# Re-dealing the steps of a period in a fused GCN and graph-attention kernel

## The chip, the cores and the metric

The kernel runs on one core of a Trainium2 chip. The metric is the device time of one execution in microseconds; before the change it is 2834.84 us, the median of 3 runs (2834.20 to 2835.28). The core has five engines with a queue of instructions each[...]: TensorE (PE; its weight loads are shown as PEld), VectorE (DVE), ScalarE (ACT), GpSimd (POOL) and SyncE (SP), which here issues every DMA.

## The reference

64 graphs of 256 nodes with 512 features, all in float32. `adj` is 256x256 for each graph. First comes a three-layer GCN with a residual and a layer norm, then a graph attention with a residual and a layer norm:

```python
h = relu(adj @ (x @ W1) + b1)
h = relu(adj @ (h @ W2) + b2)
x = layernorm(x + adj @ (h @ W3) + b3)
q, k = split(x @ Wqk);  v = x @ Wv
w = mask / sqrt(512) * rowsum(q * (adj @ (k * mask)))
x = layernorm(x + softmax(w, axis=nodes)[:, :, None] * v)
```

## The kernel before

**Tiling.** Two graphs make a pair; there are 32 pairs. Every matrix product is done in the Strassen-Winograd form of `seven` (L110): seven products of half-size blocks instead of eight, numbered 1 to 7, with sums of blocks prepared before and results combined after. In each of its seven steps a group of matmuls writes a PSUM bank; ScalarE copies partial results into `tmp` tiles, VectorE (`add`, L65) or GpSimd (`padd`, L68) makes the block sums. One bank (`x` in `seven`) is added to by products 1, 6, 5 and 3, so each of them but the first must wait until ScalarE has copied out the one before; another (`v`) is used by 7 and then by 4, and 4 must wait until VectorE has done the sum called `c22`.

**The double product.** In the attention, q and k enter only as q·k, so Wq and Wk are multiplied together once at the start (`make_m`). Then x is multiplied by that matrix and by Wv with two nested Strassen forms, 49 products of 128x128 blocks (`attention`, L512). The outer products are dealt into four groups a, b, c, d (`OUTER`, L213). The order is a and b by turns, seven steps each, and then c and d by turns (`STEPS`). The weights for this do not stay on the chip: `fetch` (L225) loads them from DRAM into a ring of 7 slots, 256 KB for a step of a, b or c, and 128 KB for one of d. Each step, after its matmuls, issues the fetch for the step seven further on (L545). The text calls these 28 steps the products p1 to p28, and the fetch for p(n) f(n).

**Periods and steps.** The work of three pairs overlaps. A period `i` runs generators that each yield after a small piece of work, and a string, `ORDER`, says which generator makes its next step (`run`, L631). There are 31 periods with `ORDER` (i from 1 to 31), one with `START` ahead of them and one with `END` behind. Every engine executes its own instructions in the order in which this string issued them, so the string is the schedule. The k-th occurrence of a letter is the k-th step of that generator, and the text names it so (F23 is the 23rd F):

- F, `front` (L402) of pair i: F1 to F7 are the seven products with W1 (L306), F8 to F11 the four groups of adj products with relu (L328, ScalarE L331), F12 to F18 the products with W2, F19 to F22 adj again, F23 to F29 those with W3. F8 first issues the load of the next pair's transposed x (L75), and F23 first issues the load of `x` (L89, 1 MB), since `put["x"] = load_x(i)` stands right before its products. 4 matmuls each.
- B, `back` (L429) of pair i-1: B1 to B7 are the seven adj products of the third layer (L364, 2 matmuls each), with the residual added by GpSimd; B8 to B12 are the layer norm and a blockwise transpose on VectorE; B13 sends the result through DRAM (`via`) to get it transposed; B14 makes block sums on GpSimd (L97).
- G, `gather`: the seven products adj·x (L364, 2 matmuls each). After G7 the load of an adj for two pairs later is issued (L84, 512 KB, in the periods up to i = 30).
- M, `attention`: M1 makes the copies and sums Z (ScalarE L521, VectorE L524), M2 and M3 the sums I (GpSimd). M4 to M17 are p1 to p14 (groups a, b), M18 to M20 VectorE work in between, M21 to M32 and M36, M37 are p15 to p28 (groups c, d). M33, M34, M38, M39 are the scores of the softmax (VectorE L560), M35 and M40 sums of v.
- E, `finish` (L592) of pair i-2: E1 transposes the scores on TensorE (L383), takes the maximum (VectorE L385), the exponential (ScalarE L388) and scales it (VectorE L390, L391). E2 transposes back (L398) and scales v. E3 to E7 are the statistics of the last layer norm, E8 to E11 its application (L617); E10 and E12 first issue a store of half a pair (L620, 512 KB).
- S, `sums`: block sums of the next pair's x (S1 to S3, GpSimd L285 to L292), the bias b3 (S4 to S7, L68) and the block sums of adj (S8 to S11).

**Buffers concerned.** 8 PSUM banks and 6 `tmp` tiles for all of this. `x` and `xm` share one buffer: `x` can be loaded once the products of `xm` (G1 to G6) are done. `v` is one buffer: its new contents (M20) must wait for the two stores.

The lines that say when a fetch and the adj load are issued, and those around E1:

```python
                fetch(at[0] + RING)
```
```python
                if n == 6:
                    put["gt"] = gt
                    if i + 2 < NPAIR:
                        aTs[i + 2] = load_adj(i + 2)
```
```python
        nc.vector.tensor_reduce(nmax, pw, AX.X, OP.max, negate=True)
        nc.scalar.activation(e, pw, AF.Exp, bias=nmax, accum_out=tot)
        nc.vector.reciprocal(rtot, tot)
        nc.vector.tensor_scalar(e, e, rtot, None, op0=OP.mult)
```

Of the kernel before, what the change touches and what calls it, by code (L numbers as in the profile page):

```python
# [20 lines left out]
def gcn_then_graph_attention(ctx: ExitStack, tc: tile.TileContext, xT, xN, adjT, mask, W1, b1, W2, b2, W3, b3,  # L21
# [570 lines left out]
    def finish(i, prev, gs=range(G)):  # L592

        r, v, w = prev
        n = len(gs)
        sm = softmax_rows(w, gs)
        yield
        s = softmax_cols(sm, gs)
        for k, g in enumerate(gs):
            for h in range(NH):  # L600
                nc.vector.scalar_tensor_tensor(v[:, g, h], v[:, g, h], s[:, h, k:k + 1], r[:, g, h, :],
                                               op0=OP.mult, op1=OP.add)
        yield
        st = small.tile([P, NH, n, 6], FP, name="st")
        mvt = small.tile([P, NH, n, 2], FP, name="mvt")
        for k, g in enumerate(gs):
            for h in range(NH):
                nc.vector.bn_stats(st[:, h, k], v[:, g, h])
                yield
        for k in range(n):  # L610
            for h in range(NH):
                nc.vector.bn_aggr(mvt[:, h, k], st[:, h, k])
        rs, nb = inv_std(mvt, n)
        yield
        for k, g in enumerate(gs):
            for h in range(NH):
                nc.scalar.activation(v[:, g, h], v[:, g, h], AF.Identity, scale=rs[:, h, k:k + 1],  # L617
                                     bias=nb[:, h, k:k + 1])
                yield
            nc.sync.dma_start(out[i, :, g * NH * D:(g + 1) * NH * D].rearrange("p (h f) -> p h f", h=NH), v[:, g])  # L620

    ORDER = ("BFFFEFFEBEFBBBFBFBBFBFEFBFBFBEBBBGFEGSFFEGGFEGEEFEMFMFFFGMMGSMEMMMMMMMMMMMSMMMMMMFSM"
             "FMMFSMMMMFFSMMMSEMMSMFMFSMSMSMM")
    START = ("BFFBBFFFBFBBBBFBBFBBBBBBBFBFBBFFBBBBBBBFFBFBBBFBFBBFBBFBBBFFBFBBBBFBBFFBFBBBBBFSBBBB"
             "SSSBBFSSBSFSBSBSBBBSBSB")
    END = ("BEEBEEBEEBBBBEBBBBEBEEBBBGGEMMBBMGGMEMGMMGMBMMMGMMMMMMMMMMMMMMMMMMMMMMMMXMMMMMXXMMYX"
# [2 lines left out]
    def run(order, **gens):  # L631
        res = {}
        for k in order + "FSBGMEXY" * 90:
            if k in gens and k not in res:
                try:
                    next(gens[k])
                except StopIteration as e:
                    res[k] = e.value
        assert len(res) == len(gens)
        return res  # L640

    def later(put, f):
        yield from f(put)
# [5 lines left out]
    for i in range(NPAIR + 1):  # L649
# [12 lines left out]
        if i == NPAIR:  # L662
            for g, k in enumerate("XY"):
                gens[k] = later(done, lambda d, g=g: finish(NPAIR - 1, d[g], [g]))
        order = START if i == 0 else ORDER if i < NPAIR else END
        res = run(order.replace(" ", ""), **gens)
# [39 lines left out]
```

## Time and profile before

| what | value |
|---|---|
| time, median of 3 runs | 2834.84 us |
| span of the profiled execution | 2832.0 us |
| granted TensorE clock, mean | 0.995 |
| instructions | 36770, of these 12688 matmuls |
| DMA, mean of the span | 142 GB/s; 328.54 MB read, 72.48 MB written |
| fetches of the ring, 256 KB | 672, median 3.3 us from issue to landing |
| load of x, 1 MB | 32, median 6.5 us |
| load of adj, 512 KB | 32, median 5.3 us |
| store of half a pair, 512 KB | 64, median 3.7 us |
| matmul 128x256, float32 | shown as 379 ns each; two such instructions for each matmul of the program |

In the profile an engine's row lists what it did, and in brackets how long it sat idle before and what released it. Since matmuls overlap in the array, the shown duration of one is longer than the distance to the next; idle time of TensorE has therefore to be read from the distances between starts. A float32 matmul of the program appears as two matmul instructions.

### The profile page before, as it was taken

The numbers are of one execution on the slowest core, as the hardware profiler recorded it, in microseconds if no ns is written. First come the engines' busy times: TensorE is split into PE (matmuls) and PEld (weight loads), VectorE is DVE, ScalarE is ACT, GpSimd is POOL, SyncE is SP. The second block draws the span as 40 slices with busy tenths as digits, with TensorE's granted clock in tenths as the row PEclk, the third lists the DMA queues.
The fourth block names the chain that finished last, engine by engine and source line by source line (L and its number), as shares of the span: only waits on it lengthen the run. The fifth ranks groups of instructions, "written<-read, shape, count | busy, mean of one in ns | idle before, by whom it ended". The sixth has DMA issues, their size and how long they took to land.

```text
span 2832.0 us, 36770 instructions
## 1 busy us (share of the span) xinstructions
PE 2740.0 (97%) x12688; PEld 2371.6 (84%) x12688; DVE 1703.6 (60%) x2898; ACT 1151.9 (41%) x1888; POOL 1786.5 (63%) x1446
## 2 busy tenths in 40 slices
PE   9999999999999999999999999999999999999996
PEld 8888888888888888888888888888888888888875
DVE  4566555665556665556655566655566655666556
ACT  2343344433444433444334444334443334443343
POOL 2656665666756666656667566666565676666663
PEclk9999999999999999999999999999999999999998
DMA  6434554344544344543445433455434455334442
GB/s 218 143 120 136 159 172 141 107 140 146 158 155 126 117 147 149 171 141 109 140 143 159 156 127 116 143 159 166 143 113 136 142 158 164 123 114 149 144 151 95
DMA packets 197752, 403.45 MB, mean 142 GB/s; under 512 B 20160, under 2 KB 57408, under 8 KB 189504
## 3 DMA queue, kind: packets, MB, share of 16 engines
q1 hardware_dynamic: 197568, 401.10, 44.5%
q8 instruction: 103, 1.69, 0.2%
q14 instruction: 81, 0.66, 0.1%
HBM read 328.54 MB, written 72.48 MB: 142 GB/s over the span
## 4 chain that ended last, share of the span: by engine, by line
PE 86%; DMA 7%; ACT 3%; DVE 3%; issue 1%; POOL 0%; SPq 0%; ACTq 0%; DVEq 0%; POOLq 0%
PE ps L306 37%; PE ps L543 18%; PE ps L328 15%; PE ps L364 14%; DMA ring<-mv 6%; DVE e L391 1%; ACT L388 1%; ACT e L388 1%; ACT tmp L126 1%; ACT tmp L117 1%; PE ps L248 1%; PE ps L398 0%; DVE gt L560 0%; DMA xT<-in_xT 0%; DVE w L97 0%
## 5 line engine op out<-in xcount | busy, mean ns | idle before, releaser
L306 PE MATMUL ps<-w_T,S 128*128 128x256 f32 x2304 | 539.7, 379 | 3.0 <-POOL S L289 1.8
L65 DVE TENSOR_TENSOR R<-ps,tmp 128x512 f32<-128x512 f32 (+1 forms) x384 | 235.4, 620 | 455.1 <-PE ps L543 350.2
L306 PEld LDWEIGHTS ps<-w_T,S 128*128 128x128 f32 x2304 | 437.8, 190 | 63.5 <-POOL S L289 3.1
L543 PE MATMUL ps<-ring,I 128*128 128x256 f32 x1792 | 435.3, 383 | 36.5 <-DMA ring<-mv 33.8
L328 PE MATMUL ps<-aT,sup 128*128 128x256 f32 x2048 | 457.7, 379 | 0.0
L328 PEld LDWEIGHTS ps<-aT,sup 128*128 128x128 f32 x2048 | 389.5, 190 | 52.4
L543 PEld LDWEIGHTS ps<-ring,I 128*128 128x128 f32 x1792 | 332.8, 190 | 107.0 <-ACT tmp L134 40.3
L65 DVE TENSOR_TENSOR sup<-ps,tmp 128x512 f32<-128x512 f32 x288 | 195.6, 686 | 279.7 <-PE ps L306 171.5
L134 ACT COPY tmp<-ps 128x512 f32<-128x512 f32 (+1 forms) x288 | 158.3, 561 | 473.6 <-PE ps L306 251.3
L68 POOL TENSOR_TENSOR I<-Z 128x384 f32<-128x384 f32 (+1 forms) x128 | 173.3, 1374 | 262.6 <-ACT Z L521 244.9
L543 PE MATMUL ps<-ring,Z 128*128 128x256 f32 x1344 | 327.7, 380 | 0.0
L68 POOL TENSOR_TENSOR tmp<-tmp,R 128x512 f32<-128x512 f32 x192 | 214.9, 1140 | 169.8 <-DVE R L580 141.5
L126 ACT COPY tmp<-ps 128x512 f32<-128x512 f32 (+1 forms) x288 | 158.1, 560 | 358.9 <-PE ps L543 173.8
L117 ACT COPY tmp<-ps 128x512 f32<-128x512 f32 (+1 forms) x288 | 158.7, 563 | 326.7 <-PE ps L364 120.2
L543 PEld LDWEIGHTS ps<-ring,Z 128*128 128x128 f32 x1344 | 256.4, 191 | 34.7
L68 POOL TENSOR_TENSOR tmp<-tmp,x 128x512 f32<-128x512 f32 x96 | 120.9, 1273 | 208.8 <-ACT tmp L134 208.8
L306 PE MATMUL ps<-w,hT 128*128 128x256 f32 x1024 | 242.1, 379 | 0.0
L331 ACT ACTIVATE hT<-ps,b 128x512 f32<-128x512 f32 x256 | 167.6, 681 | 157.5 <-PE ps L328 155.1
L68 POOL TENSOR_TENSOR x<-x,b3b 128x512 f32<-128x512 f32 x128 | 176.8, 1382 | 73.2 <-DMA x<-in_xN 63.8
L306 PEld LDWEIGHTS ps<-w,hT 128*128 128x128 f32 x1024 | 194.7, 190 | 26.5 <-DVE R L65 0.3
L285 POOL TENSOR_TENSOR S<-hT 128x512 f32<-128x512 f32 x64 | 81.8, 1279 | 202.8 <-ACT hT L331 202.8
L364 PE MATMUL ps<-T,aS 128*128 128x256 f32 x768 | 204.6, 389 | 0.0
(111 smaller groups left out, 4503.8 us busy)
## 6 DMA issues: line engine op xcount, KB each, us to landing
ring<-mv SPq DMA_DIRECT2D x672, 256.0 KB, 3.3
x<-in_xN SPq DMA_DIRECT2D x32, 1024.0 KB, 6.5
out<-v SPq DMA_DIRECT2D x64, 512.0 KB, 3.7
xT<-in_xT SPq DMA_DIRECT2D x31, 1024.0 KB, 4.8
via<-tr SPq DMA_DIRECT2D x31, 1024.0 KB, 4.3
x1T<-via SPq DMA_DIRECT2D x124, 256.0 KB, 4.7
ring<-mv SPq DMA_DIRECT2D x224, 128.0 KB, 2.9
aT<-in_adjT SPq DMA_DIRECT2D x32, 512.0 KB, 5.3
```

The lines of the kernel that those rows point to most:

```text
L65: nc.vector.tensor_tensor(o, a, b, op=OP.add)
L68: nc.gpsimd.tensor_tensor(o, a, b, op=op)
L117: nc.scalar.copy(t1, x)
L126: nc.scalar.copy(u, x)
L134: nc.scalar.copy(q, x)
L285: eng.tensor_tensor(S[2], blk(0, 0), blk(1, 0), op=sub)
L306: nc.tensor.matmul(ps[:, g], lhsT=src[n][:, c, g], rhs=w[n][:, c], start=(first and g == 0 and c == 0), stop=(g == G - 1 and c == 1), skip ...
L328: nc.tensor.matmul(ps[:, g], lhsT=C[k][c // 2][:, g, (c % 2) * P:(c % 2 + 1) * P], rhs=aT[:, k, g], start=(g == 0 and k == 0), stop=(g == ...
L331: nc.scalar.activation(hT[c // 2][:, c % 2], ps, AF.Relu, bias=b[:, c:c + 1])
L364: nc.tensor.matmul(ps[:, g], lhsT=aS[n][:, g], rhs=mov[n][:, g], start=(first and g == 0), stop=(g == G - 1), skip_group_check=True)
L388: nc.scalar.activation(e, pw, AF.Exp, bias=nmax, accum_out=tot)
L543: nc.tensor.matmul(ps[:, k], lhsT=left[n](place[o]), rhs=wt[:, k], start=(first and k == 0), stop=(k == len(outer) - 1), skip_group_check= ...
```

## The change

Only the string `ORDER` changes. It holds the same steps, each letter equally often, in another order; `START` and `END` stay.

```diff
-    ORDER = ("BFFFEFFEBEFBBBFBFBBFBFEFBFBFBEBBBGFEGSFFEGGFEGEEFEMFMFFFGMMGSMEMMMMMMMMMMMSMMMMMMFSM"
-             "FMMFSMMMMFFSMMMSEMMSMFMFSMSMSMM")
+    ORDER = ("FBFEFFEFEBBBBFBBFBFBFBFFBBBFEFBEBGFSGFFGEGFEEGEEFEFFFEMMGGMFMMFMMMMMSMSMMMMMMMMMMFMS"
+             "MMFMMMMMFMMSESMSMSMFMSMSMMMFFSM")
```

Spelled out by steps:

- *The start of the double product.* F22 and F23 now stand amid the first steps of groups a and b: G6, G7, M3, F22, M4, M5, F23, M6 to M17. Before it was F22, G6, M3, M4, G7, M5 to M17, and F23 came only after M22. With F23 the load of x goes out between the fetches f9 and f10.
- *The adj load* (behind G7) is issued before M4 instead of after it, and *the second store* (E12) before M1 instead of after M5.
- *Z and I.* M1 and M2 come after F21 instead of around F19, and M3 before F22.
- *The softmax transposes.* F1, B1, F2, E1, F3, F4, E2, F5 instead of B1, F1, F2, F3, E1, F4, F5, E2.
- *The products of the back.* B2 to B7 stand closer together: B2, B3, B4, B5, F6, B6, B7, F7 instead of B2, F6, B3, B4, B5, F7, B6, F8, B7. B8 to B13 follow earlier, and E4 to E7 (statistics of the last layer norm) later.
- *The second half of the double product.* F24 now comes before M22, F25 before M25, F27 after M34 (it was before M30), and F28 and F29 after M39 (they were after M35 and M36).
- *The sums S.* S2 comes after M10 (it was after G7) and S3 after M11 (it was after M16); S4 to S11 are dealt anew, mostly a few steps earlier or later.

## The prediction

> **What bounds the kernel now.** I read the page first: shares of the span, then the chain that ended last.
>
> ```profile
> PE 2740.0 (97%) x12688; PEld 2371.6 (84%) x12688; DVE 1703.6 (60%) x2898; ACT 1151.9 (41%) x1888; POOL 1786.5 (63%) x1446
> PE 86%; DMA 7%; ACT 3%; DVE 3%; issue 1%; POOL 0%; SPq 0%; ACTq 0%; DVEq 0%; POOLq 0%
> ```
>
> TensorE is the bound, and the change removes none of its work. What can move is the idle time, so next come the waits of TensorE alone (engine, line, waited for: total us, times, longest):
>
> ```profile
> PE ps L543 <- DMA ring<-mv: 33.8, 39, 2.3
> PE ps L398 <- DVE e L391: 22.6, 28, 3.6
> PE ps L383 <- DVE gt L560: 9.4, 3, 4.0
> ```
>
> These are understated: a 128x256 matmul is shown as 0.379 us long, but the next one starts 0.216 us after it. I therefore added up, over the whole trace, every distance between matmul starts beyond 0.216. Inside line 543 that gives 52.9 us (52 in the periods of ORDER, 1.7 for each of the 30 that load an adj); ahead of line 398 it gives 21.1 us (0.7 a period). A period has 386 matmuls of 0.216 us, 83.5 us, plus about 0.4 for the four small transposes, and lasts 86.4 on average. So about 2.5 us a period, 77 us in 31 periods, is all there is to win, and those two waits are nearly all of it.
>
> The first wait, in one period. TensorE's timeline, then SyncE's (start, us, engine, line), then a piece of the chain of waits:
>
> ```profile
> 1082.46 1.89 PE L543 MATMUL ps<-ring,Z 128*128 128x256 f32 x8
> 1085.69 1.10 PE L543 MATMUL ps<-ring,I 128*128 128x256 f32 x4 [1.34 <-DMA ring<-mv]
> 1087.60 2.69 PE L543 MATMUL ps<-ring,I 128*128 128x256 f32 x11 [0.80 <-DMA ring<-mv]
> ```
>
> ```profile
> 1077.47 0.34 SPq L230 DMA_DIRECT2D ring<-mv  x1
> 1078.37 0.33 SPq L84 DMA_DIRECT2D aT<-in_adjT  x1
> 1079.20 0.32 SPq L230 DMA_DIRECT2D ring<-mv  x1
> 1079.61 0.38 SPq L620 DMA_DIRECT2D out<-v  x1
> 1080.09 13.83 SPq L230 DMA_DIRECT2D ring<-mv  x14
> ```
>
> ```profile
> 1080.09 7.38 DMA ring<-mv
> ```
>
> The ring holds 7 slots, so fetch f(n) is issued when product p(n-7) is done, and p(n) needs it. Ahead of f9 stands an adj load (0.5 MB), ahead of f10 an output store (0.5 MB): f10, issued at 1080.09, lands 7.38 us later, while p10 wanted it earlier. Fetches that follow land 0.67 us apart and are eaten one per 0.865 us, so the stall happens once and does not come back. The last period of ORDER, which has no adj load, lost 0.33 us there.
>
> The second wait (all engines, same columns):
>
> ```profile
> 1119.46 0.59 ACT L126 COPY tmp<-ps 128x512 f32<-128x512 f32 x1 [2.87 <-PE ps L306]
> 1119.68 0.41 DVE L385 TENSOR_REDUCE nmax<-ps 2x1 f32<-2x256 f32 x1
> 1120.07 1.28 ACT L388 ACT_TABLE_LOAD   x1
> 1121.36 0.47 ACT L388 ACTIVATE e<-ps,nmax 2x256 f32<-2x256 f32 x1
> 1122.14 1.44 DVE L391 TENSOR_SCALAR e<-e,rtot 2x256 f32<-2x256 f32 x1
> 1123.73 0.25 PE L398 MATMUL ps<-ident,e 2*128 2x2 f32 x2 [0.63 <-DVE e L391]
> ```
>
> The table load starts 0.02 us after the copy of line 126 in nearly every period, at times before nmax is ready, so it waits only for its place in ScalarE's queue. That copy needs F3, the product straight ahead of the transposes.
>
> **What the Trainium skill says.** "DMA: Bandwidth & Descriptors", section Queues, rings and completion order: all that SyncE issues goes through one row of rings, taken in order on each DMA engine. The trace agrees: f10 lands 0.6 us behind the store ahead of it. "ScalarE: Activation LUTs", section What ACT_TABLE_LOAD costs: about 1283 ns, and a drain of about 1380 ns. The load is 1.28 here; no separate drain shows, so I count 1.28. "SBUF — State Buffer", section SBUF: two separate sides: VectorE and GpSimd share a port pair as an exclusive lock. That fits line 391, which takes 0.42 us at 1035.41 and 1.44 at 1122.14, beside a GpSimd add.
>
> **The change, part by part.** TensorE times below are sums of 0.216 us over the new order; "of the period" counts from its first product.
>
> *Adj load and second store.* E12 moves ahead of M1 and G7 from behind M4 to ahead of it. With the adj issue as zero: F22 runs to 1.73, p1 to 2.60 (f8), p2 to 3.46 (f9), F23 to 5.19, p3 to 6.05 (f10); p8 starts at 9.5, p9 at 10.4, p10 at 11.2. The adj landed 5.3 us after issue (median), so f8 lands near 5.9 and f9 near 6.6: both early. The store goes out some 4 us before the adj and is gone.
>
> *F23 and the x load.* F23 brings the x load (1 MB) at 3.9, between f9 and f10. Bound from below: 1 MB at 0.67 us per 256 KB is 2.7, so f10 lands at 6.6 + 2.7 + 0.7 = 10.0, over 1 us early. Bound from above: x in the trace of before lands after 5.0 to 7.9 us, and the fetch issued 2.2 us behind it lands 5.3 to 8.3 (mean 7.0) after x's issue; as adj and two fetches still stand ahead, I add 0.5: mean 3.9 + 7.5 = 11.4, worst 12.7. With 0.15 for waking that is a stall of 0 to 1.6 us, on average 0.45. I take 0.45, 13 us in 30 periods, against 52. F23's own 1.73 us gives the ring that much longer. Behind p10 the 0.67 against 0.865 holds again.
>
> *Softmax transposes.* New: F1, B1, F2, E1, F3, F4, E2; still two products, 3.46 us, between line 383 and line 398, but the copy ahead of the table load is now B1's. It ends near 3.4 us of the period, the load near 4.7, and line 383 starts at 4.3, so the load is hidden behind F2. nmax is ready 0.73 later (from the rows), at 5.05; from the exp to line 398 the rows give 1123.73 - 1121.36 = 2.37; line 398 can start at 7.4 and its place is 8.0. The 0.7 a period goes: 21 us.
>
> *F6 out of the B products.* Old: B5, F7, B6, F8, B7; new: B5, F6, B6, B7. B7 reuses the bank that VectorE must empty first (line 65, c22), which needs GpSimd's sum of B5's copy. The rows of B5 before (its matmuls end at 1041.88):
>
> ```profile
> 1042.14 0.58 ACT L134 COPY tmp<-ps 128x512 f32<-128x512 f32 x1 [1.28 <-PE ps L364]
> 1042.80 2.50 POOL L68 TENSOR_TENSOR tmp<-tmp,x 128x512 f32<-128x512 f32 x2 [5.83 <-ACT tmp L134]
> 1044.42 0.68 DVE L65 TENSOR_TENSOR r<-ps,tmp 128x512 f32<-128x512 f32 x1
> ```
>
> First GpSimd sum done 1042.80 + 1.26 = 1044.06, 2.18 after B5; then 0.1 + 0.68 + 0.15: B7 can start 3.1 after B5. Before, 4.3 us of products lay between; now 2.6. New stall: 0.5 a period, 15 us. Behind that VectorE add in its queue stand the norm's statistics and F7's sum, which F10 wants; by the same rows they end near 21.5 of the period, and F10's second product is at 22.9.
>
> *Tail.* F27's sum (VectorE) now queues behind two scores of line 560 (together 2.65 us in the trace); it ends near 81.9 and F29 wants its bank at 82.2. I allow 0.1 a period, 3 us; bounds 0 and 0.5.
>
> *Z and I sums.* M1 and M2 come later: ScalarE's first copies behind F21's activation, end of the second near 50.1 of the period, M4's use of it at 51.0; GpSimd's third sum near 55.0, M8 at 55.8. I cost them at nothing: products F22, M4 to M7 hide them.
>
> *Start of the last phase.* The scores end about 3 us earlier in the period, and END puts line 383 at its very start, where TensorE waited up to 4.0 us: minus 3 us once.
>
> The other moved steps (S1 to S11, E3 to E8, B9 to B13) I cost at nothing too: VectorE and GpSimd are busy 60% and 63% of the span, and no product of TensorE that reads what these steps make comes closer behind them than it did, or within 2 us.
>
> Sum: -(52 - 13) - 21 + 15 + 3 - 3 = -45, so 2834.8 - 45 = 2790.
>
> **The rivals.** (a) x takes the place of adj: f10 stalls near 1.5 us in every period. Then the ring gains 52 - 45 = 7 only: -7 - 21 + 15 + 3 - 3 = -13, 2822. For it: x is twice adj's size. Against: 2.6 us more lead. (b) The ring stall goes fully, as where no adj was loaded: 2790 - 13 = 2777, and 2762 if the B7 wait is hidden too. (c) Slower: x at its worst (1.9), B7 0.6, F29 0.5, and the late Z and I sums 0.5 at M4 and M8: 3.5 against 2.45 a period, 1.05 x 31 = 33 more, minus 3: 2865. For it: four thin margins (0.1 to 0.9 us). Against: a stall in one place adds slack in the next.
>
> **How the numbers follow.** Main case 0.56, (a) 0.14, (b) 0.22, (c) 0.08. The range from 2768 to 2820 takes in the main case with its bounds, most of (b), and stops short of (a)'s middle and of (c). Faster 0.88; same 0.04, between (a) and (c); slower 0.08.
>
> **What would show it.** Right: the wait of line 543 on the ring falls to some 10 us or less, that of line 398 on line 391 vanishes with the table load ahead of line 383, and a new wait of line 364 on line 65's r of 0.3 to 0.5 us appears some 31 times. Wrong: ring waits behind x as long as before, or new waits of line 543 on Z or I, or of line 306 on sup.

## The result, and the profile after

The changed kernel takes 2806.5 us (median of 4 runs, 2800.18 to 2809.06) beside 2834.52 us for the kernel before on the same chip (4 runs, 2833.10 to 2835.28): ratio 0.9898, 95% interval 0.9881 to 0.9916. It is 28 us faster; 45 us were forecast. The time lies inside the range that the forecast gave, 17 us above its single number.

The page of the changed kernel, shares of the span and of the chain that ended last:

```profile
PE 2741.9 (98%) x12688; PEld 2370.7 (85%) x12688; DVE 1718.5 (61%) x2898; ACT 1158.0 (41%) x1888; POOL 1817.1 (65%) x1446
PE 91%; DMA 3%; POOL 2%; DVE 2%; ACT 1%; issue 1%; SPq 0%; ACTq 0%; DVEq 0%; POOLq 0%
```

TensorE does the same matmuls and its share of the chain rises from 86% to 91%, as that of the DMA falls from 7% to 3%. Its waits (engine, line, waited for: total us, times, longest):

```profile
PE ps L543 <- DMA ring<-mv: 12.1, 14, 1.6
PE ps L383 <- DVE gt L560: 6.0, 3, 3.7
PE ps L398 <- DVE e L391: 5.9, 2, 3.6
PE ps L364 <- DVE r L65: 5.3, 29, 0.9
PE ps L364 <- POOL T L97: 2.6, 2, 1.8
```

Two of the three forecast signs are here: the wait of line 398 has gone from 28 times to 2, both in `END`, and line 364 waits for line 65's r 29 times instead of once. The third is just missed: the wait on the ring has fallen from 33.8 to 12.1, not to "some 10 us or less", and that small miss is a part of the answer below.

As in the prediction, the list understates, so I added up every distance between matmul starts beyond 0.216 us over both traces and put each distance to one place; below, "by distances" means this sum. The places add up to the whole difference of the two profiled executions, 2831.99 - 2798.40 = 33.6 us:

| where TensorE lost time | before | after | difference | predicted |
|---|---|---|---|---|
| inside line 543, nearly all of it for the ring | 51.7 | 19.5 | -32.2 | -39 |
| ahead of line 398 (softmax) | 21.1 | 2.8 | -18.3 | -21 |
| ahead of and in B7 (line 364) | 0 | 13.1 | +13.1 | +15 |
| ahead of F29 | 0 | 0.6 | +0.6 | +3 |
| `END`, from its line 383 on, with the wait ahead | 20.6 | 19.8 | -0.8 | -3 |
| first 80 us | -4.2 | -3.1 | +1.1 | 0 |
| all other distances | -10.2 | -7.3 | +2.8 | 0 |

(Below zero are places where small transposes take less than 0.216. Some 2.5 us of the first row, in both kernels, are waits of p11 and p12 for ScalarE's copies. In the last two rows, some 1.7 us are a stretch of half clock at 77.8 us of the changed kernel's profile, told of in the last section, and 1.7 us more stand ahead of B5.) The timed executions of the changed kernel lie up to 9 us above its profiled one, so the medians differ by 28 and not by 34. The second profile of it, in the first experiment, shows at least one thing that varies from execution to execution: the sum of the first row alone is 3.2 us more there.

**The burst after.** The burst is the run of products p1 to p14, each of which sends off a fetch. One period. TensorE's timeline:

```profile
1149.96 1.89 PE L543 MATMUL ps<-ring,Z 128*128 128x256 f32 x8
1151.69 1.89 PE L306 MATMUL ps<-w,hT 128*128 128x256 f32 x8
1153.41 3.62 PE L543 MATMUL ps<-ring,I 128*128 128x256 f32 x16
1156.87 1.89 PE L543 MATMUL ps<-ring,Z 128*128 128x256 f32 x8
1158.59 1.03 PE L543 MATMUL ps<-ring,I 128*128 128x256 f32 x4
1160.65 2.91 PE L543 MATMUL ps<-ring,I 128*128 128x256 f32 x12 [1.03 <-DMA ring<-mv]
```

and SyncE's (start, us to issue, line):

```profile
1148.46 0.34 SPq L84 DMA_DIRECT2D aT<-in_adjT  x1
1151.02 1.18 SPq L230 DMA_DIRECT2D ring<-mv  x2
1152.29 0.38 SPq L89 DMA_DIRECT2D x<-in_xN  x1
1154.47 10.30 SPq L230 DMA_DIRECT2D ring<-mv  x11
```

The adj load now goes out ahead of the burst, and no store stands in it. What stands in it is the load of x, at 1152.29, between f9 and f10. x landed 7.57 us after its issue, f10 0.66 us behind it at 1160.52, and p10, whose place was 1159.45 (1158.59 + 4 x 0.216), started at 1160.65. Over all periods but one, the stall is close to what x's landing time exceeds 6.2 us: none in the periods where x landed within 6.2, 1.04 where it took 7.2, 1.88 where it took 8.1. In the one, x took 6.4, but f10 landed 1.9 us behind it instead of 0.7, and p10 lost 1.3.

**The softmax transposes after** (all engines):

```profile
1443.48 0.59 ACT L117 COPY tmp<-ps 128x512 f32<-128x512 f32 x1 [0.28 <-PE ps L364]
1444.09 1.28 ACT L388 ACT_TABLE_LOAD   x1
1445.01 0.38 PE L383 MATMUL ps<-ident,w 128*2 128x128 f32 x2
1445.43 0.41 DVE L385 TENSOR_REDUCE nmax<-ps 2x1 f32<-2x256 f32 x1 [1.29 <-PE ps L383]
1445.88 0.47 ACT L388 ACTIVATE e<-ps,nmax 2x256 f32<-2x256 f32 x1 [0.51 <-DVE nmax L385]
1446.65 1.33 DVE L391 TENSOR_SCALAR e<-e,rtot 2x256 f32<-2x256 f32 x1
1448.78 0.28 PE L398 MATMUL ps<-ident,e 2*128 2x2 f32 x2
```

The table load starts behind B1's copy, before line 383 even runs, and the exponential follows nmax at once. e is ready at 1447.98 and wanted at 1448.78. The order of events is the predicted one, and the load still costs 1.28 us with no drain to be seen beside it.

The trace of before shows a second condition of the old wait: line 391, whose two lengths the prediction names for the lock, but not as a part of this wait. A period in which it was short, with the table load as late as ever:

```profile
1033.34 1.28 ACT L388 ACT_TABLE_LOAD   x1
1035.41 0.42 DVE L391 TENSOR_SCALAR e<-e,rtot 2x256 f32<-2x256 f32 x1
1036.31 0.28 PE L398 MATMUL ps<-ident,e 2*128 2x2 f32 x2
```

In the kernel before the wait ahead of line 398 is 0.78 to 0.81 us by distances where line 391 takes 1.43 to 1.46 (26 periods), 0.29 in the one where it takes 0.94, and 0.09 in the three where it takes 0.42 to 0.51. So the late table load cost TensorE time only where line 391 was slow as well. In the changed kernel line 391 still takes 1.33 to 1.37 in every period and the distance is 0.09: the load's new place is enough, though where line 391 was fast, the old place cost nothing either.

**B5 to B7 after** (all engines):

```profile
1454.61 0.58 ACT L134 COPY tmp<-ps 128x512 f32<-128x512 f32 x1 [1.22 <-PE ps L364]
1455.27 2.49 POOL L68 TENSOR_TENSOR tmp<-tmp,x 128x512 f32<-128x512 f32 x2 [3.06 <-ACT tmp L134]
1456.13 1.03 PE L364 MATMUL ps<-sup,aS 128*128 128x256 f32 x4
1456.57 0.69 DVE L65 TENSOR_TENSOR r<-ps,tmp 128x512 f32<-128x512 f32 x1 [0.69 <-POOL tmp L68]
1457.32 1.13 PE L364 MATMUL ps<-T,aT 128*128 128x256 f32 x4 [0.15 <-DVE r L65]
```

The chain of the prediction, link by link: B5's copy, GpSimd's sum, VectorE's line 65, B7. B7's place was 1456.13 + 0.86 = 1456.99, so it came 0.33 us late; with the first distance inside B7 it is 0.42 in each period.

### The profile page after: what moved, and what is told of

The parts are those of the page before. It is cut to its first block, busy times and chain, and to the rows that moved or that the text cites. A ratio compares the mean times of both kernels' runs of the same rounds, so it can differ in the third digit from the quotient of the medians.

```text
span 2798.4 us, 36927 instructions
## 1 busy us (share of the span) xinstructions
PE 2741.9 (98%) x12688; PEld 2370.7 (85%) x12688; DVE 1718.5 (61%) x2898; ACT 1158.0 (41%) x1888; POOL 1817.1 (65%) x1446
## 4 chain that ended last, share of the span: by engine, by line
PE 91%; DMA 3%; POOL 2%; DVE 2%; ACT 1%; issue 1%; SPq 0%; ACTq 0%; DVEq 0%; POOLq 0%
PE ps L306 39%; PE ps L543 22%; PE ps L328 16%; PE ps L364 13%; DMA ring<-mv 3%; POOL tmp L68 2%; DVE r L65 1%; ACT tmp L134 1%; PE ps L248 1%; PE ps L383 0%; PE ps L398 0%; DMA xT<-in_xT 0%; DVE w L97 0%; POOL x L68 0%; POOL T L97 0%
## 5 line engine op out<-in xcount | busy, mean ns | idle before, releaser
L306 PE MATMUL ps<-w_T,S 128*128 128x256 f32 x2304 | 547.7, 381 | 2.4 <-POOL S L289 1.9
L543 PE MATMUL ps<-ring,I 128*128 128x256 f32 x1792 | 425.1, 381 | 13.8 <-DMA ring<-mv 12.1
L134 ACT COPY tmp<-ps 128x512 f32<-128x512 f32 (+1 forms) x288 | 161.0, 559 | 541.9 <-PE ps L306 305.8
L68 POOL TENSOR_TENSOR tmp<-tmp,R 128x512 f32<-128x512 f32 x192 | 229.4, 1208 | 125.5 <-ACT tmp L134 50.6
L117 ACT COPY tmp<-ps 128x512 f32<-128x512 f32 (+1 forms) x288 | 161.2, 560 | 313.6 <-PE ps L306 133.6
L126 ACT COPY tmp<-ps 128x512 f32<-128x512 f32 (+1 forms) x288 | 158.6, 562 | 287.9 <-PE ps L306 154.9
L331 ACT ACTIVATE hT<-ps,b 128x512 f32<-128x512 f32 x256 | 175.6, 686 | 119.8 <-PE ps L328 114.4
L364 PE MATMUL ps<-T,aS 128*128 128x256 f32 x768 | 197.1, 386 | 2.6 <-POOL T L97 2.6
L68 POOL TENSOR_TENSOR tmp<-tmp,x 128x512 f32<-128x512 f32 x96 | 134.3, 1413 | 99.7 <-ACT tmp L134 99.7
L68 POOL TENSOR_TENSOR x<-x,b3b 128x512 f32<-128x512 f32 x128 | 189.4, 1489 | 0.0
```

What stands on the lines that cost most here:

```text
L68: nc.gpsimd.tensor_tensor(o, a, b, op=op)
L117: nc.scalar.copy(t1, x)
L126: nc.scalar.copy(u, x)
L134: nc.scalar.copy(q, x)
L306: nc.tensor.matmul(ps[:, g], lhsT=src[n][:, c, g], rhs=w[n][:, c], start=(first and g == 0 and c == 0), stop=(g == G - 1 and c == 1), skip ...
L331: nc.scalar.activation(hT[c // 2][:, c % 2], ps, AF.Relu, bias=b[:, c:c + 1])
```

## The experiments

No order below leaves a step out; only the order of the steps differs. "The adj part" is the earlier adj load and second store, "the tail" the end of the second half, from M29 on. Ratios are to the kernel before on the same chip, which took 2824.1 us (median) beside the first four runs told of here, 2827.5 beside the next four, 2830.0 beside the three after them and 2828.2 beside the last. Only the changed string is shown.

**The change again, and x's place.** The first run is the changed kernel once more, on the chip of the three runs that follow it.

> The changed kernel once more, to see what differs between its executions (2800 to 2809 us). Theory X (the rest of the ring's stall is set by how late the x load lands): line 543's stall inside the double product follows x's landing period by period, about landing minus 6.2 us, and a slower execution has more x loads that land after 7 us; with a median of 2806 its sum over the periods is some 24 us against 18 in the profile at hand. Theory T (slow stretches of TensorE after an idle time): the stall of line 543 stays near 18 us and matmul distances of 0.43 us in place of 0.216 make the difference.

Measured: 2803.59 us, ratio 0.9925 (0.9910 to 0.9939). The stall inside line 543 is 22.7 us by distances (0.76 a period, where the first profile had 19.5, or 0.65), and it again sits at p10 behind x. In 29 of the 31 periods it follows x's landing as before; in the other two f10 landed 2.1 us behind x, and p10 lost 1.2 and 1.4. Loads of x over 7 us are 13 here and 12 there, so the difference between the two is in part these late fetches.

If x causes it, the stall must move with x. Next, x's load is issued one step later, by F24, behind p15:

```diff
-        return (yield from support(src, wl[3], last))
+        third = support(src, wl[3], last)
+        next(third)
+        yield
+        put["x"] = load_x(i)
+        return (yield from third)
```

> The changed kernel with one edit: F23 makes its products where it does, but the x load is issued by F24, after p15. Theory X: the ring's stall of 0.6 to 0.8 us a period goes to 0.1 or less, 18 to 24 us, so some 2783 us. Rival R (thirteen fetches in a row are too many whatever else is loaded): line 543 still loses 0.5 us or more a period and the time stays within 5 us of the changed kernel. GpSimd then waits for x at S4 until some 6 us after p15; if that reaches TensorE, line 306 or 364 gets a new wait and up to 10 us of the gain are lost.

Measured: 2804.99 us, ratio 0.9934 (0.9917 to 0.9950): no gain. Its waits of TensorE have the ring on another line (the edit moves line 543 to 546):

```profile
PE ps L546 <- DMA ring<-mv: 9.6, 17, 1.0
```

This is what the rival theory forecast for the time, but not where it put the cause: p10 no longer waits, though its fetches still go out one behind the other. The stall now stands at p23, 15.9 us in all (at p10 it was 17.5 and 20.7 in the two profiles of the changed kernel), again mostly in the periods in which x landed late (7.1 us: mostly 0.8 to 0.9; 6.3 us or less: none). So x is the cause, but p15 is no better place. Without a stall, the product that needs the fetch behind x starts 7.2 us after x's issue at either place (1152.29 to 1159.45; 1168.89 to 1176.10).

**B7.** In the changed order, B7 and F7 change places:

```diff
-    ORDER = ("FBFEFFEFEBBBBFBBFBFBFBFFBBBFEFBEBGFSGFFGEGFEEGEEFEFFFEMMGGMFMMFMMMMMSMSMMMMMMMMMMFMS"
+    ORDER = ("FBFEFFEFEBBBBFBFBBFBFBFFBBBFEFBEBGFSGFFGEGFEEGEEFEFFFEMMGGMFMMFMMMMMSMSMMMMMMMMMMFMS"
```

> The changed kernel with B7 and F7 exchanged, so that 4.3 us of products lie between B5 and B7 as before the change. If the wait of line 364 on VectorE's sum costs what its rows say (0.32 us and 0.1 us for the matmul behind it, in each of 31 periods), the time falls by 13 us to some 2793 us. Rival: the wait only uses up slack, TensorE meets the same delay at the next ring fetch, and the time falls by less than 5 us.

Measured: 2793.05 us, ratio 0.9887 (0.9872 to 0.9901), 10.5 us below the changed kernel beside it. The wait of line 364 is gone and nothing comes in its place. The new wait was a real cost of the change, and avoidable.

**Only the adj load and the store.** The order of before, with G7 ahead of M4 and E12 ahead of G6; x stays behind p16:

```diff
-    ORDER = ("BFFFEFFEBEFBBBFBFBBFBFEFBFBFBEBBBGFEGSFFEGGFEGEEFEMFMFFFGMMGSMEMMMMMMMMMMMSMMMMMMFSM"
+    ORDER = ("BFFFEFFEBEFBBBFBFBBFBFEFBFBFBEBBBGFEGSFFEGGFEGEEFEMFMFFFEGMGMSMMMMMMMMMMMMSMMMMMMFSM"
```

> The kernel of before with one part of the change: G7 and its adj load ahead of M4, and the second store (E12) ahead of G6. F23 and the x load stay behind p16. If adj and store were the whole of the old stall, the 1.77 us a period of line 543 fall to 0.2 or less: minus 47 to 53 us, some 2784 us, more than the whole change gave. Rival (adj lands 5 us after its issue wherever it stands, and f8 waits for it): a stall of about 0.5 us a period stays, some 2797 us. Rival (the new place of F23 is what frees the ring): less than 15 us gained, 2820 us or more.

Measured: 2782.49 us, ratio 0.9854 (0.9839 to 0.9869), better than the whole change by 21 us. Its waits of TensorE begin:

```profile
PE ps L398 <- DVE e L391: 18.6, 23, 3.6
PE ps L383 <- DVE gt L560: 9.3, 3, 4.0
```

No wait on the ring is left in the list (0.4 us by distances; 3.0 more, 0.1 a period ahead of p11, are a wait for ScalarE), though x lands later here than in the changed kernel (7.3 us on average, up to 8.4). From x's issue (1160.69) to the product that needs the fetch behind it (1173.46) there are 12.8 us, as F24, F25, F26 and F27 stand between.

**How much of it is the store.** The same, with E12 left behind M5:

```diff
-    ORDER = ("BFFFEFFEBEFBBBFBFBBFBFEFBFBFBEBBBGFEGSFFEGGFEGEEFEMFMFFFEGMGMSMMMMMMMMMMMMSMMMMMMFSM"
+    ORDER = ("BFFFEFFEBEFBBBFBFBBFBFEFBFBFBEBBBGFEGSFFEGGFEGEEFEMFMFFFGMGMSMEMMMMMMMMMMMSMMMMMMFSM"
```

> As the kernel with adj and store earlier, but the second store stays behind M5, between f9 and f10; only G7 and its adj load go ahead of M4. If the store counted as much as its 0.5 MB: f10 lands some 1.4 us later than without it, still within the time that p10 leaves (f10 of the kernel with both moved was never late), so a stall of 0 to 0.3 us a period and 2783 to 2792 us. Rival (the store is what held f10 up): a stall of 1 us or more stays, 2812 us or more.

Measured: 2806.5 us, ratio 0.9924 (0.9906 to 0.9942), between the two forecasts; stall inside line 543 0.85 a period. Of the 1.7 a period before, the adj load was worth some 0.9, and the store, taken out after it, some 0.8. The store alone was not tried.

**Only the softmax transposes.** The order of before with its first eight letters changed, and the same on top of the adj part:

```diff
-    ORDER = ("BFFFEFFEBEFBBBFBFBBFBFEFBFBFBEBBBGFEGSFFEGGFEGEEFEMFMFFFGMMGSMEMMMMMMMMMMMSMMMMMMFSM"
+    ORDER = ("FBFEFFEFBEFBBBFBFBBFBFEFBFBFBEBBBGFEGSFFEGGFEGEEFEMFMFFFGMMGSMEMMMMMMMMMMMSMMMMMMFSM"
```

> The kernel of before with one part of the change: the period begins F1, B1, F2, E1, F3, F4, E2, F5, and B2 follows. Theory (the table load of the exponential is hidden behind F2): the wait of line 398 on line 391 is gone in the 30 periods that have it, 0.6 us each by the distances between matmul starts in the two traces, so 17 us less. Rival (the wait comes from VectorE's or GpSimd's backlog at the period's start, and the change only removes it together with the other moves): less than 6 us.

> The kernel of before with two parts of the change: adj load and store earlier, and the softmax transposes. Left out: F23 with the x load in the burst, the tight B products, the new places of Z, I and the sums. If the two gains add (42 us measured for the first part, 17 us expected for the second, in different places of the period) this runs 59 us below the kernel of before and well below the changed kernel; if VectorE or GpSimd at the start of the period carries a delay on, less than 50 us.

Measured: 2836.77 us, ratio 1.0031 (1.0021 to 1.0042) alone; 2791.95 us, ratio 0.9874 (0.9859 to 0.9889), with the adj part, which by the ratios is 0.0020 (6 us) slower than the adj part without it, a difference about as wide as its uncertainty. Both miss their forecast gain. This move, without the rest of the change, gains nothing, and alone it costs time. In the waits of TensorE of the run with the transposes alone:

```profile
PE ps L383 <- DVE gt L560: 26.0, 31, 4.0
```

Line 398 waits no longer, but line 383, now one product (1.73 us) earlier in the period, waits for the scores in nearly every period. By distances that is 21 us, where the transposes win 18 ahead of line 398, and 4 more are lost ahead of F6; with the adj part it is 22, 14 and 4. The parts of the change don't add up one by one.

**F23 back.** In the changed order, F23 goes back behind M22, and F24 behind M23, so that x is out of the burst:

```diff
-    ORDER = ("FBFEFFEFEBBBBFBBFBFBFBFFBBBFEFBEBGFSGFFGEGFEEGEEFEFFFEMMGGMFMMFMMMMMSMSMMMMMMMMMMFMS"
-             "MMFMMMMMFMMSESMSMSMFMSMSMMMFFSM")
+    ORDER = ("FBFEFFEFEBBBBFBBFBFBFBFFBBBFEFBEBGFSGFFGEGFEEGEEFEFFFEMMGGMFMMMMMMMSMSMMMMMMMMMMMFSM"
+             "FMFMMMMMFMMSESMSMSMFMSMSMMMFFSM")
```

> The changed kernel with one part undone: F23 and its x load go back behind M22, and F24 behind M23, as before the change. Theory X (the x load amid p3 to p14 is what the ring still waits for): line 543's stall of 0.6 to 0.8 us a period goes to 0.1, about 20 us less than the changed kernel. Rival (without F23's 1.7 us amid the products the ring runs dry on rate alone): the stall stays at 0.5 us or grows, and nothing is gained.

Measured: 2816.88 us, ratio 0.9960 (0.9945 to 0.9975), slower than the change, which neither theory had. The ring stall is gone, as theory X said, but line 543 waits for something else. Its waits of TensorE, first line:

```profile
PE ps L543 <- POOL I L68: 23.0, 31, 0.8
```

and the same in its timeline:

```profile
1161.40 1.26 POOL L68 TENSOR_TENSOR I<-I,Z 128x512 f32<-128x512 f32 x1
1162.72 1.99 PE L543 MATMUL ps<-ring,I 128*128 128x256 f32 x8 [0.74 <-POOL I L68]
```

M8 needs GpSimd's third I sum, which the change makes late, since M1 and M2 come later. F23's 1.73 us of products ahead of M6 is what hid it. In the changed order F23 can't simply leave the burst.

**Transposes and tail together.** Line 383 waits for M38's and M39's scores; in the change these stand ahead of F28 and F29. Three runs take the order of before with the change's second half from M29 on: with adj part and transposes, with the transposes alone, and by itself.

```diff
-    ORDER = ("BFFFEFFEBEFBBBFBFBBFBFEFBFBFBEBBBGFEGSFFEGGFEGEEFEMFMFFFGMMGSMEMMMMMMMMMMMSMMMMMMFSM"
-             "FMMFSMMMMFFSMMMSEMMSMFMFSMSMSMM")
+    ORDER = ("FBFEFFEFBEFBBBFBFBBFBFEFBFBFBEBBBGFEGSFFEGGFEGEEFEMFMFFFEGMGMSMMMMMMMMMMMMSMMMMMMFSM"
+             "FMMFSMMMMFMMSMSEMSMFMSMSMMMFFSM")
```

> The order of before with three parts of the change: adj load and second store ahead of M4 (as in the run with these alone), softmax transposes as in the change (F1, B1, F2, E1), and the second half from M29 on dealt as in the change (M38 and M39 ahead of F28 and F29). F23 with the x load stays behind M22, B5 to B7 and the Z and I copies stay as before. Theory P (the parts add once the scores come early): the adj part alone gave 42 us (2827.5 to 2782.5 or 0.985); the softmax transposes then give 0.58 a period more, 17 us: about 59 us below before, ratio 0.979, about 2766 on a chip where before takes 2826. Ring stall in line 543 about 0.1 a period, line 383 waits for line 560 in the last period only, no wait of line 364 on r near B7. Theory Q (a late x load and the new tail collide, or line 383 still waits for the scores): no better than the adj part alone, ratio 0.985 or more.

> The order of before with the softmax transposes of the change and its second half from M29 on, and nothing else: adj load and store stay amid the fetches. Theory P: line 383 waits for the scores no more in each period (26 us in the run with the transposes alone), the 0.7 a period ahead of line 398 is gone, 17 us below before, ratio 0.994; ring stall stays 1.7 a period. Theory Q: the scores still come too late, or the ring stall grows by what was won: ratio 0.999 to 1.003.

> The order of before with only its second half from M29 on dealt as in the change. Theory P: by itself the tail gives next to nothing, as line 398 still waits for the table load behind the copy of F3: ratio 0.998 to 1.000, line 398 waits as before (about 20 us in the list of waits). Theory Q: the tail itself is what pays (the scores earlier, 3 us at the start of the last phase) or costs (F29 behind its bank, 0.1 to 0.5 a period, 3 to 15 us): ratio 0.994 or 1.003.

Measured: 2793.96 us, ratio 0.9877 (0.9862 to 0.9892); 2836.8 us, ratio 1.0026 (1.0014 to 1.0037); 2839.74 us, ratio 1.0031 (1.0019 to 1.0043). All three miss the first theory and lie in the range of the second. Line 383 has stopped waiting within the periods, as that theory said, but the waits of TensorE of the first of the three now begin with F29:

```profile
PE ps L306 <- DVE sup L65: 14.2, 20, 2.1
```

Without the one wait that the kernel before has too (2.1 us), that is 12 us in the list and some 17 by distances, 0.55 us a period. This is the term that the prediction allowed 0.1 for and that is next to zero in the changed kernel. Two periods of this one run, one with the stall and one without (all engines):

```profile
1174.93 3.18 POOL L68 TENSOR_TENSOR tmp<-tmp,R 128x512 f32<-128x512 f32 x3
1176.23 0.69 DVE L65 TENSOR_TENSOR R<-ps,tmp 128x512 f32<-128x512 f32 x1 [1.13 <-POOL tmp L68]
1178.07 1.26 POOL L68 TENSOR_TENSOR x<-x,b3b 128x512 f32<-128x512 f32 x1
1178.10 1.79 DVE L560 SCALAR_TENSOR_TENSOR gt<-R,mask_s,gt 128x512 f32<-128x512 f32 x1
1179.82 1.20 DVE L560 SCALAR_TENSOR_TENSOR gt<-R,mask_s,gt 128x512 f32<-128x512 f32 x1
1180.95 0.68 DVE L65 TENSOR_TENSOR sup<-ps,tmp 128x512 f32<-128x512 f32 x1
1181.69 1.13 PE L306 MATMUL ps<-w_T,hT 128*128 128x256 f32 x4 [0.90 <-DVE sup L65]
...
1088.99 1.27 POOL L68 TENSOR_TENSOR tmp<-tmp,R 128x512 f32<-128x512 f32 x1
1090.71 0.68 DVE L65 TENSOR_TENSOR R<-ps,tmp 128x512 f32<-128x512 f32 x1
1092.67 0.75 DVE L560 SCALAR_TENSOR_TENSOR gt<-R,mask_s,gt 128x512 f32<-128x512 f32 x1
1092.83 1.72 POOL L68 TENSOR_TENSOR x<-x,b3b 128x512 f32<-128x512 f32 x1
1093.36 1.74 DVE L560 SCALAR_TENSOR_TENSOR gt<-R,mask_s,gt 128x512 f32<-128x512 f32 x1
1095.03 0.68 DVE L65 TENSOR_TENSOR sup<-ps,tmp 128x512 f32<-128x512 f32 x1
1096.31 1.03 PE L306 MATMUL ps<-w_T,hT 128*128 128x256 f32 x4
```

Two things come together. In the first period GpSimd is behind in its queue, and VectorE waits 1.13 us for its `tmp` ahead of the sum at 1176.23; in the second that sum follows without a wait. So VectorE reaches the scores late: in the stalled periods of this run the first score starts 0.3 to 1.7 us before F28, in the others 1.9. Then the late score meets GpSimd's next add, which starts 0.03 us ahead of it, and takes 1.79 us; in the second period the score starts 0.16 us ahead and takes 0.75, and it is GpSimd's add that takes 1.72 instead of 1.26. The Trainium skill has the second thing so ("SBUF — State Buffer", section SBUF: two separate sides): the port pair that the two share is an exclusive lock, and whichever starts first holds it for its whole instruction. The trace agrees in the direction: whichever of the two starts second takes longer, the score by 1.04 us and the add by 0.46. F27's sum stands in VectorE's queue behind both scores, and starts 2.85 us after the first one here, against 2.36 there.

The margin where nothing is late is 0.6 us (in a period of the changed kernel without stalls the sum ends at 82.27, counted from the first product, and F29 starts at 82.87). In the period shown VectorE is 1.1 us late and the scores cost 0.49 more: 1.1 + 0.5 - 0.6 = 1.0, and F29's stall by distances is 1.07. In the 30 periods behind the first, all 21 slow first scores of this run stand before a stalled F29 (16.0 us together), none of the 9 fast ones; in the two other runs it is so for 17 and 14 slow ones. In the changed kernel the first score was fast in 29 of these 30 periods, and the one slow one has a 0.76 us stall.

**The sum between the scores.** If the place behind both scores is what makes F27's sum late, nothing of TensorE's order need change. In the last order, F27 is issued between M33 and M34, so that VectorE does F27's sum after one score:

```diff
-             "FMMFSMMMMFMMSMSEMSMFMSMSMMMFFSM")
+             "FMMFSMMMMFMMSMSEMSFMMSMSMMMFFSM")
```

> The order of the run with adj part, softmax transposes and the new second half, with F27 issued between M33 and M34 instead of behind M34, so that VectorE does F27's sum after the first score and not after both. TensorE's order is unchanged. Theory P (in that run F29 waited 0.55 a period only because VectorE's sum of F27 stood behind two scores, of which the first took 1.79 us instead of 0.75 in two periods of three): the wait of line 306 on sup is gone, 16 us less: ratio 0.982, some 2779 beside 2830. Theory Q (the sum is late for another cause, or the scores that now come later hold up M38, M39 and line 383): ratio 0.986 or more, with a wait of line 383 on line 560 in many periods or line 306 waiting as before.

Measured: 2774.56 us (5 runs, 2771.83 to 2778.72), ratio 0.9808 (0.9794 to 0.9823): the first score is still slow in 20 of 30 periods, and F29 waits in none to speak of (0.3 us in all). Its page:

```profile
PE 2734.4 (99%) x12688; PEld 2371.0 (85%) x12688; DVE 1684.9 (61%) x2898; ACT 1155.6 (42%) x1888; POOL 1801.8 (65%) x1446
PE 97%; DVE 2%; DMA 0%; POOL 0%; issue 0%; ACT 0%; SPq 0%; ACTq 0%; DVEq 0%; POOLq 0%
```

This order, which has only the adj part, the transposes and the tail of the change, with F27's place mended, beats both kernels: about 54 us below before, where the change brought 28. TensorE is 97% of the chain; a period takes 84.34 us on average, with 83.9 of matmuls and small transposes by the prediction's count.

## Why the prediction was right, and where it was off

**The bound and the two waits: right.** Nothing but the distances between TensorE's matmuls moved, and the two waits that the prediction named fell by 50.5 us together (32.2 + 18.3); 17 us of it was handed back, 13 of these at B7, as listed.

**Adj load and store: right, and its size too.** Taken out of the burst alone they leave 0.01 a period of waiting for the ring, of some 1.7: both fetches early and the store "gone", as the step said. It went by 5.3 us for adj's landing; with nothing queued ahead of it adj lands after 3.3 (median). That error was on the safe side.

**The x load: mechanism right, mis-sized.** The step took 0 to 1.6 us and on average 0.45; it is 0.65 in the profile of the changed kernel and 0.76 in the second (0.57 and 0.67 at p10 alone). The means were right: the step had f10 land 7.5 us after x's issue and p10 wanting it 7.3 after; measured are 7.3 (x after 6.6 on average, f10 0.7 behind it) and 7.2. That the first mean fits is partly luck. The step added 0.5 for the adj load and the fetches ahead of x, but x landed 6.6 us after its issue in both kernels. What made up for it is the fetch behind x: 128 KB in the kernel before, landing 0.35 behind x, and 256 KB here, landing 0.7 behind. The term that was mis-sized is the average over the spread: x took 5.3 to 8.1 us, an early one wins nothing and a late one is paid in full, so the mean stall is well above the stall of a mean landing. A fetch that lands some 2 us behind x, in one or two periods of an execution, was in no term.

**Softmax transposes: right in the changed kernel, for a reason that the prediction did not see.** The wait ahead of line 398 fell by 18.3 us, not 21; each period keeps the 0.09 that it also had before where line 391 was fast. But the step that costed it took the scores as ready when line 383 came earlier. With the tail of before they are not: the move alone costs 9 us. In the change it pays because M38 and M39 come earlier, and the prediction valued that part of the tail at 3 us, once.

**B7: right.** +13.1 for +15, 0.42 a period for 0.5, by the chain as worked out; exchanging B7 and F7 gave 10.5 us back.

**F29: right about the risk, wrong about its kind.** It was costed as a thin but steady margin, 0.1 a period. It is rather a switch: nothing while GpSimd keeps up, and 0.7 to 0.8 on average in a period where it does not (16.0 / 21, 9.6 / 14). In the changed kernel it stood well in 29 of 30 periods. The prediction had cited the lock for line 391 and did not apply it to line 560.

**Z and I sums at nothing: right, and thin.** The step gave M8 0.8 us of margin, with F22, M4 to M7 and F23 ahead. Without F23's 1.73 us that would be a wait of 0.9; with F23 moved back, M8 waited 1.0 in each period. The step named "products F22, M4 to M7" as what hides it; F23 belonged in that list.

**The start of the last phase: wrong.** Line 383 of `END` does wait 0.8 instead of 4.1 us, as forecast. Line 398 behind it waits 2.4, where it waited 2.8 before. But then line 364 waits for GpSimd's T of line 97 (3.0 by distances, 2.6 in the list of waits; 0 before) and takes most of the gain back: -0.8 instead of -3. Why T comes late there was not tried.

**The rivals.** (a), x takes the place of adj, gave 2822: x's stall is 0.65 to 0.76 and not 1.5. (b), the ring stall goes fully, is what the adj part does by itself, with x out of the burst. (c) did not come, but three of the places that it names beside x turned out to be real costs in one order or the other: B7 in the change, F29 with the new tail, M8 with F23 back.

**Open.** Why GpSimd keeps up ahead of the scores in the changed kernel and mostly does not in the three runs with its new tail was not tried; the steps S2, S3 and S5, which are GpSimd's, stand elsewhere in the two, but no run moved these alone. The place of x's load is not the reason: with F23 moved back, x is loaded behind p16 as in those three runs, and only 2 of 31 first scores were slow. The changed kernel's profiled execution took 2800.18 us, some 6 less than the median; the landings of x and of the fetch behind it can make up a part of this, the rest is open.

## What to carry to other kernels

When loads share one queue with a ring that is eaten at a set pace, count for each large load the time from its issue to the use of the fetch right behind it, and hold that against the worst landing time seen, not the mean: here 7.2 us was too little for 1 MB and 12.8 enough. A change made of many moves should be taken apart even where it wins: here three of its parts, with one step moved besides, give nearly twice what the whole gives, one part costs time without another, and one hides a wait that a third made. Where the length of an instruction is in doubt, as where VectorE and GpSimd meet, put the result that TensorE waits for ahead of it in its queue.

## What the runs showed of the hardware that was not expected

- After waits of TensorE, 7 to 10 matmuls sometimes follow 0.427 us apart instead of 0.216. In the changed kernel it happens after 2.24 us of idling that end at 77.3 us into the span and costs some 1.7 us; in the kernel before, the same 2.24 us that end at 77.4 have no such effect. The granted clock in the traces shows it: from 77.8 to 81.2 us its mean is 0.51 in the changed kernel and 1.00 in the kernel before. The Trainium skill ("TensorE: Matmul & The Clock Gate", section HAM oscillation — how this bites in real kernels) puts the limit for such idling at about 3.4 us; here 2.2 us was at times enough, and at times not.
- Which of the two it is goes by the idle time within fixed steps. In each of the 14 kept traces, all changes of the granted clock lie whole multiples of 3.41 us apart. Cut into steps of this length, from 20 us to 2690 us, the traces have 14 steps in which TensorE idled 2.11 us or more by distances, in one wait or in several, and each was followed by a step at half the clock; none was after 2.01 us or less; of the three steps between (2.07, 2.07 and 2.10) two were. In the kernel before, the border of a step cuts the wait at 77 us into 1.5 and 0.7; in the changed kernel it lies whole within one.
- A load of 1 MB from DRAM took from 5.3 to 8.1 us from issue to landing in otherwise equal periods of the changed kernel, and a 256 KB fetch issued 2.2 us behind it landed 0.6 to 0.8 us after it, whatever it took, in 30 of 31 periods (1.9 in the other).
- The same VectorE instruction, 128x512 with two inputs (line 560), takes 0.75 or 1.79 us, by whether it starts 0.16 us before or 0.03 us after a sum of GpSimd.
